# Layer 1's gathers contract over all 128 partitions, on a query block that holds rounded values in one half and the rests in the other

## The chip, the cores and the metric

The kernel runs on one core of a Trainium2 chip. A core has a matrix engine (TensorE, PE in the profile, its weight loads listed apart as PEld), a vector engine (VectorE, DVE), a scalar engine (ScalarE, ACT), GpSimd (POOL) and a queue engine for transfers (SyncE, SP). The metric is the device time of one execution in microseconds (us), the median of several runs. Lower is better.

## The reference, cut to what matters

Four layers, each `x = x + gnn(relu(layernorm(x)))`, work on x of shape 128 x 64 x 256: 128 graphs of 64 nodes with 256 features. The change touches layer 1 alone, an attention over 512 edges that are the same for all graphs:

```python
Xq = (H @ W_lin.T).reshape(bt, n, h, dh)      # 4 heads of 64
Xv = (H @ W_val.T).reshape(bt, n, h, dh)
Qs = Xq[:, src]                               # 512 edges
Kt = Xq[:, dst]
e = jnp.einsum('behd,hd->beh', jax.nn.leaky_relu(Qs + Kt, 0.2), a)
e = e + jnp.log(A0[src, dst] + EPS)[None, :, None]
attn = softmax of e over the edges that share a source node
Y = segment_sum(attn * Xv[:, dst], src)       # back to 64 nodes
return Y @ W_out.T
```

For every graph the kernel thus needs, per edge, the sum of two query rows. It gets it with a matrix multiplication by a table of zeros, ones and twos with one column per edge.

## The kernel before, in words

The 8192 tokens (128 graphs of 64 nodes) lie in 64 tiles of 128 tokens, so a tile holds two graphs: one on partitions 0 to 63, one on 64 to 127. Four tiles are a chunk, two tiles a pair `q`, eight pairs a group. Layer 1 loops over the 32 pairs in `edges(q)`. For each of the two tiles of a pair it does this:

- `gather(it)` takes the tile's query block and multiplies it with `sd_hot` [128, 512], the table of edges, which stands twice, once for each half of the partitions. For each of two halves `c` of the 256 features a PSUM pair of banks gets one bank per graph (`par`). ScalarE evicts the pair with a ReLU into `lr` (L1131).
- `project(it + 2)` makes the query block of the tile two further on: eight passes on TensorE at L1090, four into a bank `p` for 256 query features and 4 sums per head (`QS` = 260), four into a bank `pv` for the values. The products are in fp32, which TensorE does in two recorded passes each. The gather's are in fp32r, one pass, which rounds; so the query is split into a rounded piece and the rest, both fp32r, and both are gathered. ScalarE writes the rounded piece `xq[:, 0, :]` by a cast from PSUM (L1098), VectorE the rest `xq[:, 1, :]` by a subtraction (L1099). GpSimd adds the 4 columns of head sums of both pieces into `head_sums` (L1103).
- `joined` lets VectorE fold the two feature halves (`scalar_tensor_tensor`, L1137).

Between the tiles stand, in every even pair, the transposes of the next chunk's normalised rows (`turn1`, L173, two halves of four transposes with a PSUM bank each, evicted by ScalarE at L176), and at the end of a pair the score of the pair before it (L1146). After eight pairs `linear_part` (L1162) adds the part of the leaky ReLU that is linear, from `head_sums`, and the softmax of that group of pairs (`edge_softmax`) is worked off in small steps on VectorE during the next pairs, one to three steps a pair. The last eight pairs also carry the multiplication with the values (`weigh`, `put_out`).

PSUM has eight banks: two pairs for the gathers (`pair_bank`), and four single ones (`bank`). Of the four, one holds a group's scores, one the values `pv` of two tiles, and the others go to `p` and to the transposes in turn.

The order on each engine is laid out by a planner when the program is built; `late(...)` marks an instruction that keeps its place in the program's order. Buffers that matter: `xq` has 4, `lr` 6, `head_sums` 2.

A matmul on 64 partitions uses half the rows of TensorE's array, and two on opposite halves run side by side. That is the form of the gathers here: for each feature half, the two pieces one after the other accumulate in PSUM, and the two graphs run side by side.

Of the kernel before, what the change touches and what calls it, by code (L numbers as in the profile page):

```python
# [9 lines left out]
F32 = mybir.dt.float32  # L10
# [4 lines left out]
ALU = mybir.AluOpType  # L15
AX = mybir.AxisListType

P = 128
T = 64
D = 256  # L20
HEADS = 4
# [10 lines left out]
def gnn_stack_kernel(ctx: ExitStack, tc: tile.TileContext, a: dict, out: bass.AP):  # L32
    nc = tc.nc
# [10 lines left out]
    def bank():  # L44
        return psums["now"].tile([P, 512], F32, tag="bank", name="bank", bufs=psums["banks"])

    def pair_bank():
        return psums["now"].tile([P, 2, 512], F32, tag="pair", name="pair", bufs=2)
# [29 lines left out]
    def late(ins):  # L78

        tc.keep_in_program_order(ins)  # L80
# [192 lines left out]
    sd_hot = tabs.tile([P, E], F32R, tag="sd_hot", name="sd_hot")  # L273
# [205 lines left out]
    with ExitStack() as l0:  # L479
# [39 lines left out]
        with ExitStack() as conv:  # L519
# [38 lines left out]
            for h in range(2):  # L558
                r = slice(h * T, (h + 1) * T)
# [4 lines left out]
            p = bank()  # L564
# [366 lines left out]
        for slot in range(len(tasks) + 2):  # L931
# [26 lines left out]
            if new:  # L958
                next(one)
                flight.append((new, one))  # L960
                at, k = new[0], new[2]
# [38 lines left out]
    with ExitStack() as l1:  # L1000
# [4 lines left out]
        def pool(name, bufs):  # L1005
            return l1.enter_context(tc.tile_pool(name=name, bufs=bufs, reuse_waits="tile"))
# [12 lines left out]
        sgp = pool("sgp", 2)  # L1019
# [7 lines left out]
        QS = D + HEADS  # L1027
# [10 lines left out]
        hTs, queries, values, scores, waiting = {}, {}, {}, {}, []  # L1038
        sums_of, values_bank = {}, [None]
# [37 lines left out]
        def project(it):  # L1077

            n, i = it // 4, it % 4
            if i == 0:  # L1080
                kept = n >= NCH - KEPT
                values[n] = (later_pools["vk"] if kept else vp).tile([P, 4, D], F32, tag="xv", name="xv")
            p = bank()
            if not i % 2:
                values_bank[0] = bank()
            pv = values_bank[0]
            parts = ((p[:, :QS], slice(0, QS)), (pv[:, i % 2 * D : (i % 2 + 1) * D], slice(QS, QS + D)))
            for o, cols in parts:
                for k in range(2):
                    ins = nc.tensor.matmul(  # L1090
                        o, hTs[n][:, k, i * P : (i + 1) * P], wlv[:, k, cols], start=k == 0, stop=k == 1
                    )
                    if k == 0:
                        late(ins)


            xq = queries[it] = t3.tile([P, 2, QS], F32R, tag="xq", name="xq")
            nc.scalar.copy(xq[:, 0, :], p[:, :QS])  # L1098
            late(nc.vector.tensor_tensor(xq[:, 1, :], p[:, :QS], xq[:, 0, :].bitcast(F32), ALU.subtract))  # L1099
            g, at = it // 16, it % 2 * 32 + it % 16 // 2 * HEADS  # L1100
            if g not in sums_of:
                sums_of[g] = sgp.tile([P, T], F32, tag="head_sums", name="head_sums")
            nc.gpsimd.tensor_tensor(  # L1103
                sums_of[g][:, at : at + HEADS], xq[:, 0, D:].bitcast(F32), xq[:, 1, D:].bitcast(F32), ALU.add
            )
            if i % 2:
                (nc.vector.tensor_copy if i > 2 else nc.scalar.copy)(
                    values[n][:, i - 1 : i + 1, :].rearrange("p i d -> p (i d)"), pv
                )
            if i == 3 and n < NCH - KEPT:  # L1110
                nc.sync.dma_start(out=xv_mem[n], in_=values.pop(n))

        def gather(it):

            lrs = []
            for c in range(2):
                p = pair_bank()
                for piece in range(2):
                    for par in range(2):
                        r = slice(par * T, (par + 1) * T)  # L1120
                        ins = nc.tensor.matmul(  # L1121
                            p[:, par, :],
                            queries[it][r, piece, c * P : (c + 1) * P],
                            sd_hot[r, :],
                            start=piece == 0,
                            stop=piece == 1,
                        )
                        if not par and not piece:
                            late(ins)
                lr = lrp.tile([P, 2, E], F32, tag="lr", name="lr")  # L1130
                nc.scalar.activation(lr, p, AF.Relu)  # L1131
                lrs.append(lr)
            return lrs
# [23 lines left out]
        def linear_part(g):  # L1157

            s = sums_of.pop(g)
            for par in range(2):  # L1160
                r = slice(par * T, (par + 1) * T)
                ins = nc.tensor.matmul(  # L1162
                    scores[g][r, :], s[r, :], sd_hot[r, :].bitcast(F32), start=False, stop=True, skip_group_check=True
                )
                if not par:
                    late(ins)
# [266 lines left out]
        def next_score():  # L1433
            q, lrs = waiting.pop(0)
            score(q, lrs)
            if q % 8 == 7:
                linear_part(q // 8)
                behind.append(edge_softmax(q // 8))
# [7 lines left out]
        def edges(q):  # L1446

            n, odd = q // 2, q % 2
            it = 2 * q
            halves = gather(it)  # L1450
            last_out()
            if it + 2 < NT:
                project(it + 2)
# [9 lines left out]
            for _ in range(2 if odd else 1):  # L1463
                step_behind()
            halves = gather(it + 1)
            last_out()
            if it + 3 < NT:
                project(it + 3)
# [18 lines left out]
        for it in range(2):  # L1487
            project(it)
# [765 lines left out]
```

## Time and profile before

| | |
|---|---|
| median of 3 runs | 1962.27 us (1961.59 to 1963.83) |
| the profiled execution | 1963.89 us, of which the span of instructions is 1962.1 us |
| layer 1's gathers, first and last start | 1256.0 and 1518.4 us of the span |
| gather matmuls (L1121) | 512, of 64 rows and 512 columns |
| projections (L1090) | 480 recorded passes, mean 393 ns each |
| cast of the query (L1098, ScalarE) | 64, mean 381 ns |
| subtraction (L1099, VectorE) | 64, mean 420 ns |
| fold (L1137, VectorE) | 64, mean 1299 ns |
| ReLU of the gathered rows (L1131, ScalarE) | 128, mean 1022 ns |
| head sums (L1103, GpSimd) | 64, from 191 to 1173 ns |

How to read the lines: a timeline line gives the start and the length in us of a run of equal instructions, the engine, the source line, the operation, the tile it writes and those it reads, the shape, the count, and in brackets the idle time of the engine ahead of it and what ended that. Matmuls overlap, so the time that a run of them takes is the distance to the start of the next run rather than its length. A group line ends in busy time, mean length in ns, and idle time ahead of the group.

### The profile page before, as it was taken

The numbers are of one execution on the slowest core, as the hardware profiler recorded it, in microseconds if no ns is written. First come the engines' busy times: TensorE is split into PE (matmuls) and PEld (weight loads), VectorE is DVE, ScalarE is ACT, GpSimd is POOL, SyncE is SP. The second block draws the span as 40 slices with busy tenths as digits, with TensorE's granted clock in tenths as the row PEclk, the third lists the DMA queues.
The fourth block names the chain that finished last, engine by engine and source line by source line (L and its number), as shares of the span: only waits on it lengthen the run. The fifth ranks groups of instructions, "written<-read, shape, count | busy, mean of one in ns | idle before, by whom it ended". The sixth has DMA issues, their size and how long they took to land. (4 is left out here: it accounts for less than half of the span.)

```text
span 1962.1 us, 25581 instructions
## 1 busy us (share of the span) xinstructions
PE 1930.9 (98%) x9406; PEld 1388.7 (71%) x9406; DVE 1305.4 (67%) x2458; ACT 1145.3 (58%) x2153; POOL 459.6 (23%) x614
## 2 busy tenths in 40 slices
PE   9999999999999999999999999999999999999998
PEld 7777478866678874788666888766656775534787
DVE  8774675574475567765654755657766777787887
ACT  4353775564565547665654656567666556592554
POOL 3000031040030011320400200256665420000574
PEclk9999999999999999999999999999999999999999
DMA  7512000010010044000100100441333841022112
GB/s 267 178 59 97 0 22 1 1 44 0 1 43 1 1 161 140 22 1 0 44 0 1 43 1 17 165 137 68 111 134 124 318 159 57 1 65 86 44 65 87
DMA packets 63870, 135.61 MB, mean 69 GB/s; under 512 B 6656, under 2 KB 41344, under 8 KB 61440
## 3 DMA queue, kind: packets, MB, share of 16 engines
q1 hardware_dynamic: 59808, 124.33, 18.4%
q0 software_dynamic: 3328, 9.44, 1.3%
q8 instruction: 74, 1.21, 0.2%
q14 instruction: 52, 0.43, 0.1%
q10 hardware_dynamic: 608, 0.20, 0.1%
HBM read 87.55 MB, written 46.40 MB: 68 GB/s over the span
## 5 line engine op out<-in xcount | busy, mean ns | idle before, releaser
L767 ACT ACTIVATE gate<-gate,bias 128x256 f32<-128x256 f32 (+2 forms) x368 | 247.2, 678 | 176.0 <-DVE gate L783 94.1
L739 PE MATMUL pa<-xop,sih 128*128 128x256 f32 (+2 forms) x1056 | 342.4, 417 | 4.6 <-DVE gate L793 4.4
L739 PEld LDWEIGHTS pa<-xop,sih 128*128 128x128 f32 x1056 | 198.4, 190 | 75.8 <-issue 18.9
L739 PE MATMUL pc<-xop,wih 128*128 128x256 f32 (+2 forms) x736 | 251.1, 423 | 0.0
L783 DVE TENSOR_TENSOR gate<-pb,gate 128x256 f32<-128x256 f32 (+2 forms) x184 | 87.5, 475 | 224.5 <-PE pb L739 152.3
L739 PE MATMUL pa<-lstm_h,shh 128*128 128x256 f32 (+1 forms) x672 | 212.7, 398 | 0.0
L739 PEld LDWEIGHTS pc<-xop,wih 128*128 128x128 f32 x736 | 139.8, 190 | 51.2 <-issue 22.5
L800 DVE TENSOR_TENSOR gate<-pc,gate 128x256 f32<-128x256 f32 (+2 forms) x184 | 87.4, 475 | 111.9 <-PE pc L739 111.4
L1131 ACT ACTIVATE lr<-pair 128x1024 f32<-128x1024 f32 x128 | 124.1, 1022 | 63.7 <-PE pair L1121 35.1
L739 PEld LDWEIGHTS pa<-lstm_h,shh 128*128 128x128 f32 x672 | 127.7, 190 | 30.2
L739 PE MATMUL pc<-lstm_h,whh 128*128 128x256 f32 (+1 forms) x448 | 141.8, 398 | 0.0
L782 ACT COPY gate<-pa 128x256 f32<-128x256 f32 (+2 forms) x184 | 76.1, 413 | 85.6 <-PE pa L739 85.1
L1090 PE MATMUL bank<-wlv,hT 128*128 128x260 f32 x480 | 120.2, 393 | 0.0
L793 DVE TENSOR_TENSOR gate<-pa,gate 128x256 f32<-128x256 f32 (+2 forms) x184 | 87.4, 475 | 41.4 <-PE pa L739 40.7
L767 ACT ACTIVATE gate<-pa,bias 128x256 f32<-128x256 f32 (+2 forms) x184 | 93.9, 510 | 30.8 <-PE pa L739 29.0
L1090 PEld LDWEIGHTS bank<-wlv,hT 128*128 128x128 f32 x480 | 86.3, 189 | 31.4 <-issue 14.7
L787 ACT COPY gate<-pa 128x256 f32<-128x256 f32 (+2 forms) x184 | 75.3, 409 | 56.3 <-PE pa L739 55.3
L739 PE MATMUL pa<-xop,wih 128*128 128x256 f32 (+1 forms) x320 | 101.6, 399 | 1.3 <-ACT xop L718 1.2
L739 PE MATMUL pb<-xop,wih 128*128 128x256 f32 (+1 forms) x320 | 100.6, 398 | 0.0
L739 PEld LDWEIGHTS pc<-lstm_h,whh 128*128 128x128 f32 x448 | 85.1, 190 | 20.1
L506 POOL TENSOR_TENSOR shh<-whh 128x512 f32<-128x512 f32 x6 | 7.8, 1294 | 378.9 <-DMA whh<-in_WhhT 321.0
L790 ACT COPY gate<-pc 128x256 f32<-128x256 f32 (+2 forms) x136 | 57.9, 426 | 53.1 <-PE pc L739 52.4
(377 smaller groups left out, 3968.9 us busy)
## 6 DMA issues: line engine op xcount, KB each, us to landing
field<-keep SPq DMA_DIRECT2D x4, 2304.0 KB
wih<-in_WihT SPq DMA_DIRECT2D x8, 1024.0 KB
xres<-in_x SPq DMA_DIRECT2D x16, 512.0 KB
xa<-xres POOLq DMA_DIRECT2D x16, 512.0 KB, 7.9
dense<-field SPq DMA_DIRECT2D x4, 2048.0 KB
xin<-xb SPq DMA_DIRECT2D x16, 512.0 KB
h<-xb SPq DMA_DIRECT2D x16, 512.0 KB
xin<-in_x SPq DMA_DIRECT2D x15, 512.0 KB
```

Source lines behind the costliest of these rows:

```text
L506: keep(nc.gpsimd.tensor_tensor(o, x, y, op))
L739: ins = nc.tensor.matmul(p[:, : self.N], weights[kind, self.phase](k, q), x[k], start=first_ and kind == "ih", stop=kind == "hh" or not se ...
L767: nc.scalar.activation(out, in_, AF.Tanh if q == 2 else AF.Sigmoid, bias=bias[:, self.w - 1, 2 * q + j : 2 * q + j + 1],)
L782: nc.scalar.copy(blk[0, 0], pa[:, :N])
L783: nc.vector.tensor_tensor(blk[0, 0], pb[:, :N], blk[0, 0], ALU.add)
L787: nc.scalar.copy(blk[1, 0], pa[:, :N])
L790: (nc.vector.tensor_copy if not self.t and self.w > 1 else nc.scalar.copy)(blk[1, 1], pc[:, :N])
L793: nc.vector.tensor_tensor(blk[1, 1], pa[:, :N], blk[1, 1], ALU.add)
L800: nc.vector.tensor_tensor(blk[1, 0], pc[:, :N], blk[1, 0], ALU.add)
L1090: ins = nc.tensor.matmul(o, hTs[n][:, k, i * P : (i + 1) * P], wlv[:, k, cols], start=k == 0, stop=k == 1)
L1131: nc.scalar.activation(lr, p, AF.Relu)
```

## The change

A query block still has two parts, but they are now one per graph rather than one per piece. The part of the first graph (`par` 0) holds that graph's rounded values in its own half of the partitions, 0 to 63, and the rests of the same values in the other half, 64 to 127; the part of the second graph holds them the other way round. Because the table of edges stands in both halves, one matmul over all 128 partitions sums the rounded values and the rests of one graph at once, so four matmuls of 128 rows take the place of eight of 64.

To fill the block, ScalarE casts the PSUM bank into both parts (260 elements become 520), and VectorE then overwrites the foreign half of each part with the rests: two subtractions on 64 partitions each, whose result is written to the other half of the partitions than the one it was read from. The head sums are kept as they are in the two parts (GpSimd copies 2 x 4 columns in place of an addition of 4), `head_sums` is twice as wide, and the linear part contracts over 128 partitions too.

```diff
             xq = queries[it] = t3.tile([P, 2, QS], F32R, tag="xq", name="xq")
-            nc.scalar.copy(xq[:, 0, :], p[:, :QS])
-            late(nc.vector.tensor_tensor(xq[:, 1, :], p[:, :QS], xq[:, 0, :].bitcast(F32), ALU.subtract))
+            nc.scalar.copy(xq, p[:, :QS].unsqueeze(1).to_broadcast([P, 2, QS]))
+            for par in range(2):
+                own, other = (slice(h * T, (h + 1) * T) for h in (par, 1 - par))
+                late(nc.vector.tensor_tensor(
+                    xq[other, par, :], p[own, :QS], xq[own, par, :].bitcast(F32), ALU.subtract
+                ))
             g, at = it // 16, it % 2 * 32 + it % 16 // 2 * HEADS
             if g not in sums_of:
-                sums_of[g] = sgp.tile([P, T], F32, tag="head_sums", name="head_sums")
-            nc.gpsimd.tensor_tensor(
-                sums_of[g][:, at : at + HEADS], xq[:, 0, D:].bitcast(F32), xq[:, 1, D:].bitcast(F32), ALU.add
-            )
+                sums_of[g] = sgp.tile([P, 2, T], F32, tag="head_sums", name="head_sums")
+            nc.gpsimd.tensor_copy(sums_of[g][:, :, at : at + HEADS], xq[:, :, D:].bitcast(F32))
...
                 p = pair_bank()
-                for piece in range(2):
-                    for par in range(2):
-                        r = slice(par * T, (par + 1) * T)
-                        ins = nc.tensor.matmul(
-                            p[:, par, :],
-                            queries[it][r, piece, c * P : (c + 1) * P],
-                            sd_hot[r, :],
-                            start=piece == 0,
-                            stop=piece == 1,
-                        )
-                        if not par and not piece:
-                            late(ins)
+                for par in range(2):
+                    ins = nc.tensor.matmul(
+                        p[:, par, :], queries[it][:, par, c * P : (c + 1) * P], sd_hot, start=True, stop=True
+                    )
+                    if not par:
+                        late(ins)
...
                 ins = nc.tensor.matmul(
-                    scores[g][r, :], s[r, :], sd_hot[r, :].bitcast(F32), start=False, stop=True, skip_group_check=True
+                    scores[g][r, :], s[:, par, :], sd_hot.bitcast(F32), start=False, stop=True, skip_group_check=True
                 )
```

## The prediction

> **What bounds the kernel now.** I read the page first: TensorE (PE) is busy for 98% of the span at full granted clock, and nothing on the chain that ended last touches layer 1. So layer 1 counts as far as it shifts PE's row.
>
> ```profile
> PE 1930.9 (98%) x9406; PEld 1388.7 (71%) x9406; DVE 1305.4 (67%) x2458; ACT 1145.3 (58%) x2153; POOL 459.6 (23%) x614
> ```
>
> Then the timeline of PE over one pair of tiles. Its lines are merged, so I read the start of one to the start of the next.
>
> ```profile
> 1382.52 1.06 PE L1146 MATMUL bank<-lr,afield 128*32 128x512 f32 x8
> 1383.51 1.21 PE L1121 MATMUL pair<-sd_hot,xq 64*128 64x512 f32 x8
> 1384.65 2.01 PE L1090 MATMUL bank<-wlv,hT 128*128 128x260 f32 x8
> 1386.49 1.29 PE L173 MATMUL bank<-ident,h 128*128 128x128 f32 x8
> 1387.71 1.20 PE L1121 MATMUL pair<-sd_hot,xq 64*128 64x512 f32 x8
> 1388.85 2.01 PE L1090 MATMUL bank<-wlv,hT 128*128 128x260 f32 x8
> 1390.79 1.06 PE L1146 MATMUL bank<-lr,afield 128*32 128x512 f32 x8
> ```
>
> A gather G (L1121) takes 1.14 us, a score S 0.99. A projection P takes 1.84 between a gather and the transposes T, 1.94 between a gather and a score. The chain of waits prices the same 128-row passes, undisturbed, in layer 4:
>
> ```profile
> 1837.02 0.87 PE pair L1958 x8
> 1837.90 3.50 PE bank L51 x16
> ```
>
> That is 0.218 us a pass and 0.109 a transpose. P's eight passes are 1.74, so P pays 0.10 on entry from the gather's 64-row shape, and 0.10 more when it leaves for another shape. By the same count a gather is 0.10 + four row-tiled pairs + 0.10, a pair 0.234.
>
> Next the timelines of ScalarE, VectorE, the weight loads and (last line, a later pair) PE:
>
> ```profile
> 1384.34 1.94 ACT L1131 ACTIVATE lr<-pair 128x1024 f32<-128x1024 f32 x2 [1.14 <-PE pair L1121]
> 1386.17 0.38 ACT L1098 CAST xq<-bank 128x260 fp32r<-128x260 f32 x1
> 1386.58 0.43 DVE L1099 TENSOR_TENSOR xq<-bank,xq 128x260 fp32r<-128x260 f32 x1 [1.42 <-ACT xq L1098]
> 1387.13 0.42 PEld L173 LDWEIGHTS bank<-ident,h 128*128 128x128 f32 x4 [0.27 <-issue]
> 1469.85 0.63 PE L173 MATMUL bank<-ident,h 128*128 128x128 f32 x4 [0.55 <-DVE xq L1099]
> ```
>
> The second half of T (call it T2) starts 0.11 us after the subtraction ends, and the last line names that subtraction: T2 needs the PSUM bank that the query leaves. So in a pair with transposes (every even one) a chain over ScalarE and VectorE holds PE already.
>
> Last the busy time by stage, for three pairs in which a softmax is worked off, and one without (columns: length, then PE, weight loads, DVE, ACT, POOL):
>
> ```profile
> 1336.87:1345.14 8.27, 8.21 (x52) 5.31 (x48) 7.10 (x15) 6.66 (x9) 4.20 (x6) 1.00 0.19 63
> 1345.14:1352.28 7.14, 7.14 (x45) 4.38 (x42) 7.11 (x10) 5.84 (x9) 5.42 (x6) 1.00 0.18 73
> 1352.28:1360.55 8.27, 8.21 (x53) 5.31 (x49) 7.48 (x17) 5.65 (x8) 4.49 (x8) 1.00 0.20 66
> 1376.37:1383.51 7.14, 7.14 (x44) 4.39 (x41) 3.84 (x5) 5.00 (x7) 6.69 (x10) 1.00 0.30 91
> ```
>
> VectorE is full (7.11 of 7.14) in the second of them.
>
> **The change, part by part.** *Gathers.* Eight 64-row matmuls become four of 128 rows, of P's own shape. No row shows a 128-row fp32r pass of 512 columns. Lower bound 0.216 (P's slot, an equal stream), upper 0.234 (the pair, which already streams 128 partitions of fp32r at once); I take 0.225. The shape changes G to P, P to G and T to G vanish; S to G and P to S stay. A pair without T goes from 7.14 to 1.00 + 1.74 + 0.90 + 1.84 + 1.00 = 6.48 (-0.66); one with T (0.87) would go from 8.27 to 7.35 (-0.92). Fifteen of each, 0.66 for pair 30 and 0.3 for the last, which only gathers: -24.7 us.
>
> The Trainium skill ("TensorE: Matmul & The Clock Gate", Part 3, The mechanism) speaks against this: weight loads overlap running matmuls only where the row groups differ, as they do between the present half tiles. By that rule each 128-row pass would pay its 0.19 us load as well, four a gather, some 48 us over 63 gathers, an estimate. But P's slot of 0.218 leaves no room for a load of 0.19 in front of each pass, so I let loads hide.
>
> *Subtraction.* One 128-partition instruction (0.43, the next starting 0.345 behind it) becomes two on 64 partitions across halves. These rows, by shape, say that half the partitions save nothing, and what halves of other quadrants do:
>
> ```profile
> L2079 DVE COPY field<-bank 64x256 f32<-64x256 f32 x1 | 0.4, 417 | 1.1 <-PE bank L2073 1.1
> L790 DVE COPY gate<-pc 128x256 f32<-128x256 f32 x36 | 14.9, 414 | 2.1 <-PE pc L739 1.8
> 147.63 0.45 DVE L253 TENSOR_TENSOR bdH<-bank,anT 64x64 f32<-64x64 f32 x2
> ```
>
> The two halves at L253 take 0.206 and 0.228 and together 0.45, so they do not overlap, and 0.013 lies between. Bounds for the next full instruction: 0.085 before the second half's end (as now), or 0.013 behind it; I take the latter, by the rows of halves. VectorE gains 2 x 0.443 - 0.345 = 0.54 us a tile (lower bound 0.345). The skill ("VectorE: DVE Perf Modes", Two Vector instructions with no wait between them) holds any instruction whose start quadrant differs from the last one's, so that fold too; no row here shows a full instruction behind a shifted half.
>
> *Cast.* 260 to 520 elements: 0.38 to 0.60, by the 128x512 copy from PSUM at L1107 (0.588). ScalarE has room (5.00 + 0.43 of 6.48).
>
> *T2.* First fold-relu starts 0.83 behind the gather (stays: the second pass now begins 0.325 in, before 0.34), cast 1.83 later, then 0.60 + 0.03 + 0.87 + 0.11: T2 at 4.27 instead of 1387.13 - 1383.51 = 3.62. The pair then ends after 0.44 + 0.90 + 1.84 + 1.00 = 8.45: +0.18 instead of -0.92. So 1.10 is lost in each of 15 pairs: +16.5. Should T2 be given the bank that T's first half leaves, it waits for that copy (till about 4.1) and 2.5 us of this come back.
>
> *VectorE in the softmax pairs.* From the subtraction at 1332.80 to that at 1355.37 it idles only 1.03 (1343.22 to 1344.25, for a projection). Its 21.5 of work gain 6 x 0.54: 24.8, begun 3.28 into the stretch, which makes T2 of the fourth pair 3.28 + 24.8 + 0.98 = 29.0 instead of 26.15. After it 0.48 is saved. The four pairs grow by 2.4 where the sums above give -1.0: 3.4 lost, in two groups of eight pairs; in the third the values' matmuls lengthen PE's row (the pair from 1474.5 takes 11.9) and I take 1.5. +8.3, and 0.3 in the second pair, where the layer-0 outputs load VectorE.
>
> *Small ones.* The first gather waits for both halves where half of it ran ahead: 0.5. The linear part stays two column halves side by side (1.01 now): 0, bounds 0.1 either way, three in the loop. POOL's sum becomes a copy of 8 elements, 0.2 to 1.16 us like now; POOL's fullest pair has 6.69 of 7.14, its neighbour 6.19 of 8.26, and its normalised rows are wanted half a chunk later; if that cover went, T's first half would be late. DMAs and SP's queue are untouched.
>
> Sum: -24.7 + 16.5 + 8.3 + 0.3 + 0.5 = +0.9. The profiled execution took 1963.9 (span 1962.1), which would be 1964.8; it stood 1.6 over the median of 1962.27, so I say 1963.2. A measurement of this kernel tells about 0.2%, 3.9 us, from no change.
>
> **The rivals.** *Faster:* VectorE isn't the bound. For: its order may be laid out anew, with scans in gaps; against: the 7.11 of 7.14. Without the 8.3, with a 0.216 pass (63 x 0.036 = 2.3) and the cheaper bank (2.5): 1950; with the 8.3 alone gone 1955. If T2 didn't wait either, 1938.
>
> *Slower:* VectorE binds wider. One mechanism, decided from about 0.4 us more lost per pair in 12 softmax pairs than I count: the exponential (ScalarE, L1181) sits ahead of a cast and waits for VectorE, so the delays add. The idle 1.03 stays in three groups (3), the third group costs as much as the others (1.9), the pass is 0.234 (2.3): 1970 to 1972.
>
> *The pass isn't single.* A 128-row fp32r pass that costs what fp32 passes of 512 columns cost (57.8 us for 128 at L51, 0.45): 63 x 0.9 = 57 more, 2018. Against: the pairs stream the same bytes in 0.234.
>
> **How the numbers follow.** No measurable change 0.35; faster 0.28 (0.02 of it 1938); VectorE wider 0.33; double pass 0.04. The range leaves out the double pass, the 1938 and the tails: 1949 to 1976.
>
> **What would show it.** Right: gathers at 0.9 to 1.0 us, P at 1.74 before a gather, T2 starting near 4.3 behind its gather on "DVE xq", pairs without T near 6.5, VectorE without idle in the softmax pairs. Wrong: a T2 that doesn't wait, or pairs without T above 7.

## The result and the profile after

The changed kernel takes 1966.1 us (median of 22 runs, 1963.5 to 1972.5) against 1961.8 us (22 runs, 1961.0 to 1964.9) before: a ratio of 1.0022, 95% interval 1.0016 to 1.0028, or 3.1 to 5.5 us slower. The prediction was 1963.2, in a range of 1949 to 1976. The profiled execution took 1968.6 us with a span of 1966.8.

The page's row of busy times:

```profile
PE 1914.2 (97%) x9150; PEld 1393.2 (71%) x9150; DVE 1344.5 (68%) x2522; ACT 1156.8 (59%) x2153; POOL 457.2 (23%) x614
```

TensorE has 16.7 us less work than before (1930.9), VectorE 39.1 us more. TensorE's work fell and the span didn't: what was saved is idle time now. The timeline of one even pair of tiles shows where (start, length, engine, line, operation; in brackets the idle time ahead and what ended it), first PE, then ScalarE, then VectorE:

```profile
1388.88 1.06 PE L1142 MATMUL bank<-lr,afield 128*32 128x512 f32 x8
1389.88 1.20 PE L1121 MATMUL pair<-sd_hot,xq 128*128 128x512 f32 x4
1390.91 1.90 PE L1090 MATMUL bank<-wlv,hT 128*128 128x260 f32 x8
1392.65 0.60 PE L173 MATMUL bank<-ident,h 128*128 128x128 f32 x4
1394.03 0.63 PE L173 MATMUL bank<-ident,h 128*128 128x128 f32 x4 [0.78 <-ACT hT L176]
1394.41 1.17 PE L1121 MATMUL pair<-sd_hot,xq 128*128 128x512 f32 x4
1395.42 1.91 PE L1090 MATMUL bank<-wlv,hT 128*128 128x260 f32 x8
1397.26 1.07 PE L1142 MATMUL bank<-lr,afield 128*32 128x512 f32 x8
...
1392.52 0.60 ACT L1098 CAST xq<-bank 128x520 fp32r<-128x520 f32 x1
1393.29 0.60 ACT L176 ACTIVATE hT<-bank 128x512 f32<-128x512 f32 x1 [0.17 <-PE bank L173]
...
1393.15 0.86 DVE L1101 TENSOR_TENSOR xq<-bank,xq 64x260 fp32r<-64x260 f32 x2 [0.65 <-ACT xq L1098]
1394.05 1.29 DVE L1133 SCALAR_TENSOR_TENSOR lr<-lr,fold 128x1024 f32<-128x1024 f32 x1
```

A gather now takes 1.03 us (1389.88 to 1390.91) where it took 1.14. The second half of the transposes T (T2) starts 4.15 us behind its gather where it started 3.65 behind, after 0.78 us of waiting. It waits for ScalarE's copy of T's first half (L176), which ends at 1393.89, and not for the subtractions, which end at 1394.01, only 0.02 ahead of it: its weight load starts 0.11 us behind the copy's end, as before the change it started 0.11 behind the subtraction's. So the planner has given T2 the bank that T's first half leaves.

The timeline of the softmax pairs 12 and 13 (PE):

```profile
1357.20 1.90 PE L1090 MATMUL bank<-wlv,hT 128*128 128x260 f32 x8
1360.08 0.63 PE L173 MATMUL bank<-ident,h 128*128 128x128 f32 x4 [0.98 <-DVE xq L1101]
1361.48 0.63 PE L173 MATMUL bank<-ident,h 128*128 128x128 f32 x4 [0.78 <-ACT hT L176]
...
1370.74 0.52 PE L1195 MATMUL bank<-ident,e 128*128 128x128 f32 x3 [2.06 <-DVE e L1189]
```

and the busy time by stage, one line per pair 10 to 13 (length, then PE, weight loads, DVE, ACT, POOL):

```profile
1340.26:1349.64 9.38, 7.86 (x45) 5.35 (x41) 9.11 (x17) 7.13 (x9) 3.02 (x4) 1.00 0.19 57
1349.64:1356.16 6.52, 6.52 (x36) 4.61 (x32) 6.28 (x9) 6.15 (x9) 5.62 (x7) 1.00 0.20 80
1356.16:1365.74 9.58, 7.82 (x45) 5.27 (x41) 9.36 (x15) 5.94 (x8) 4.77 (x5) 1.00 0.19 57
1365.74:1374.96 9.22, 7.16 (x41) 4.92 (x37) 8.37 (x15) 5.34 (x7) 6.29 (x11) 1.00 0.14 58
```

VectorE fills the even ones (9.11 of 9.38, 9.36 of 9.58). It now holds PE at three places: T (0.98), the projection ahead of the score (0.74 in pair 10), and the transposes of the softmax itself (L1195), which stand still for 2.06 us until VectorE has multiplied `e` with the reciprocals (L1189). From the first gather to pair 30's, PE stands still for 20.8 us in waits of over 0.15 us where it stood still for 2.6: 11.8 of them end with ScalarE's copy (L176), 3.7 with a subtraction and 4.3 with `e`.

Taking the starts of the gathers from the trace, pair by pair, before and after differ so (us; "undisturbed" means without a stretch of reduced clock, which comes below):

| part | predicted | measured |
|---|---|---|
| first gather with pairs 0 and 1 | +0.3 | +0.1 |
| 7 odd pairs without softmax work | -4.6 | -4.2 |
| 7 even pairs without softmax work | +1.3 | +0.9 |
| softmax pairs 10 to 13 | +2.4 | +3.5 |
| softmax pairs 18 to 21 | +2.4 | +3.5 |
| pairs 24 to 29 (values) | +0.1 | -1.1 |
| pair 30, last gather and end of layer 1, undisturbed | -1.0 | -0.5 |
| sum (of the unrounded rows) | +0.9 | +2.0 |

The row of pair 30 is taken against the second profile of before, below; in the first one a ReLU (L1131) holds a gather of pair 30 for 0.72 us, and from pair 30 to the end of layer 1 it takes 2.3 us more. The second profile of the same kernel, below, gives the same numbers to 0.05 in the first four rows and in that of the pairs 24 to 29, and +3.7 for the second softmax group. The rest of the 4.3 us isn't in any row. Two things bear on it. First, the profiles shift against each other ahead of layer 1, where no instruction differs: by 5.2 us in the first profile after (one VectorE instruction of layer 0, L852 at 1097.41, took 4.82 us there instead of 1.33), by 0.2 the other way in its repetition, by up to 1.8 between two profiles of before. Second, the granted clock: over 22 executions after, its mean is 0.9981, over the 27 executions of before that ran beside the later experiments 0.9996. After's times go with it: 1964.7 (median of 5) at 0.999, 1966.0 (13) at 0.998, 1969.2 (2) at 0.997, 1972.5 at 0.996; one run at 1.000 took 1966.2. A mean lower by 0.0015 is at most some 3 us of TensorE's time at full speed, worked out as 0.0015 x 1965. It doesn't say where in the kernel the clock was low: in the first profile after, the two stretches at half clock lie in layer 0, behind the long L852 (from 1104.2 us), and at the very end of the span (from 1964.3), none in layer 1.

### The profile page after: what moved, and what is told of

Same layout as the page of the kernel before. It is cut to its first block, busy times and chain, and to the rows that moved or that the text cites. A ratio compares the mean times of both kernels' runs of the same rounds, so it can differ in the third digit from the quotient of the medians.

```text
span 1966.8 us, 25221 instructions
## 1 busy us (share of the span) xinstructions
PE 1914.2 (97%) x9150; PEld 1393.2 (71%) x9150; DVE 1344.5 (68%) x2522; ACT 1156.8 (59%) x2153; POOL 457.2 (23%) x614
## 3 DMA queue, kind: packets, MB, share of 16 engines
q8 instruction: 72, 1.18, 0.3%
## 5 line engine op out<-in xcount | busy, mean ns | idle before, releaser
L1090 PE MATMUL bank<-wlv,hT 128*128 128x260 f32 x480 | 114.8, 382 | 1.8 <-DVE xq L1101 1.8
```

The costliest lines, as they stand in the source:

```text
L1090: ins = nc.tensor.matmul(o, hTs[n][:, k, i * P : (i + 1) * P], wlv[:, k, cols], start=k == 0, stop=k == 1)
```

## The experiments

**The changed kernel and the kernel before once more.** Nothing is edited; these say how far two profiles of the same kernel differ.

> The changed kernel once more, unaltered. Theory (the sum of the prediction): inside layer 1's loop, from the first gather to the last, it takes 0 to 2 us more than before, whatever the run. Of the 4.7 us of span that the first profile shows, 5.2 had gathered before the first projection of layer 1, 4.2 of it at one VectorE instruction of layer 0 (L852, 4.82 us instead of 1.33). If that was chance, this profile has L852 near 1.3 us there and a median 1962 to 1964; rival: the changed kernel brings it on in every run, L852 is long again, and the median is 1965 to 1967.

> The kernel before once more, unaltered: 1962 to 1963, a ratio of 1.000, and a second trace of it. Question to it: does the load of the values that holds PE for 1.2 to 2.5 us near the end of layer 1 in the changed kernel's traces (at 1566 to 1570) also hold it here in some runs, and does the clock fall to half inside layer 1? Theory: neither (both come from the changed order).

Measured: 1966.4 after, 1.0018 [1.0009, 1.0027]; 1962.1 before, 0.9999 [0.9990, 1.0008]. The loop comes out as expected, and L852 is short again (1.27 us), so its 4.8 us were chance; but the median is the rival's and not the 1962 to 1964 that was to go with a short L852. From the first gather to pair 30's, the two profiles after take 252.1 and 252.3 us, the two of before 250.9 and 250.9. In the repetition after, the clock falls inside layer 1. Busy time by stage around pair 20 of that profile (the column behind the five engines is the granted clock):

```profile
1418.00:1420.00 2.00, 1.18 (x6) 0.70 (x4) 1.97 (x4) 2.00 (x3) 0.60 (x2) 1.00 0.37 35
1420.00:1422.00 2.00, 1.05 (x9) 0.87 (x9) 1.93 (x5) 0.60 (x2) 1.23 (x1) 1.00 0.58 227
1422.00:1424.00 2.00, 2.00 (x8) 1.60 (x7) 1.90 (x5) 1.76 (x3) 0.00 (x0) 0.61 0.00 0
1424.00:1426.00 2.00, 2.00 (x7) 1.59 (x6) 1.93 (x5) 1.30 (x2) 1.24 (x1) 0.53 0.00 0
```

and its timeline of PE there:

```profile
1420.17 0.63 PE L173 MATMUL bank<-ident,h 128*128 128x128 f32 x4 [0.98 <-DVE xq L1101]
1421.57 0.63 PE L173 MATMUL bank<-ident,h 128*128 128x128 f32 x4 [0.78 <-ACT hT L176]
1421.96 1.64 PE L1121 MATMUL pair<-sd_hot,xq 128*128 128x512 f32 x4
1423.39 3.13 PE L1090 MATMUL bank<-wlv,hT 128*128 128x260 f32 x8
1426.45 1.06 PE L1142 MATMUL bank<-lr,afield 128*32 128x512 f32 x8
```

PE is idle for 1.8 of four microseconds, then runs at about half clock: the projection at 1423.39 takes 3.06 us to the next start where it takes 1.84 elsewhere. The clock's record shows half speed for 3.4 us. Pair 20 grows by 1.6 to 11.2 us, but pair 21 gives 1.4 of it back, because VectorE has caught up by then (its wait at L1195 falls from 2.2 to 0.8): among VectorE's waits the fall is nearly free. A second fall, from 1565.8 us, follows a wait for the load of the values:

```profile
1565.99 1.99 PE L1312 MATMUL pair<-att,xv_in 64*64 64x64 f32 x64 [2.45 <-DMA xv_in<-xv]
```

From pair 30 on the repetition takes 2.7 us more to the end of layer 1 than the first profile, 1.3 of it in this longer wait (2.45 for 1.18), which leaves 1.4 for the fall. The same two waits at pair 20 stand in the first profile after without a fall, so a wait of that size allows it and doesn't force it (the last section says what goes with a fall). Neither profile of before has such a stretch in layer 1; but the load of the values holds PE for 1.39 us (at 1564.74) in the second of them too, so that wait, against what was expected, isn't of the changed order.

**One half of the change alone.** `gather_only` has the new gathers and linear part on the block that the old preparation leaves, so a matmul sums other pieces than it should:

```diff
-            nc.scalar.copy(xq, p[:, :QS].unsqueeze(1).to_broadcast([P, 2, QS]))
-            for par in range(2):
...
+            nc.scalar.copy(xq[:, 0, :], p[:, :QS])
+            late(nc.vector.tensor_tensor(xq[:, 1, :], p[:, :QS], xq[:, 0, :].bitcast(F32), ALU.subtract))
```

> The 128-row gathers with the old preparation of the query (one cast of 260, one subtraction on 128 partitions): the part that saves, alone. Its gathers add up the wrong values; nothing else is changed. Theory: the transposes' second half starts near 3.6 us behind its gather as before, pairs with transposes take 7.8 instead of 8.27, pairs without 6.5 instead of 7.14, so 15 x 0.47 + 15 x 0.66 + 1 = 18 us less than before: 1944 (1940 to 1949). Rival, the saving isn't in the shape of the matmuls or is lost elsewhere than in the preparation: 1958 to 1966.

`prep_only` keeps the old gathers and head sums and prepares the block as the change does, with the wide cast and two subtractions, but each writes its own half, so the values are those of before:

```diff
+            nc.scalar.copy(xq, p[:, :QS].unsqueeze(1).to_broadcast([P, 2, QS]))
+            for par in range(2):
+                own = slice(par * T, (par + 1) * T)
+                late(nc.vector.tensor_tensor(
+                    xq[own, 1, :], p[own, :QS], xq[own, 0, :].bitcast(F32), ALU.subtract
+                ))
```

> The old 64-row gathers behind a preparation of the new cost: the cast writes both parts (520 elements), and the subtraction is two instructions on 64 partitions each (written to the half they are read from, since the old gathers need the rests there). The part that costs, alone. Theory: the second half of the transposes starts 0.65 later in 15 pairs (10 us), VectorE holds the softmax pairs of three groups for 4 more, the first gather for 0.5: 1976 (1971 to 1981). Rival, the preparation is hidden: 1961 to 1966.

Measured: `gather_only` 1951.7, 0.9939 [0.9925, 0.9953]; `prep_only` 1982.9, 1.0105 [1.0090, 1.0120]. From first gather to pair 30's they differ from before by -13.2 and +19.8. Both times lie above their ranges: each half of the change moves the time the way that was said of it, but the gathers alone bring less than expected and the preparation alone costs more, and together the two come to +1.2 where their sum is +6.6. The even pair of `gather_only` says why, in the timeline of PE:

```profile
1287.93 1.20 PE L1117 MATMUL pair<-sd_hot,xq 128*128 128x512 f32 x4
1288.97 1.90 PE L1090 MATMUL bank<-wlv,hT 128*128 128x260 f32 x8
1290.71 0.60 PE L173 MATMUL bank<-ident,h 128*128 128x128 f32 x4
1291.57 0.63 PE L173 MATMUL bank<-ident,h 128*128 128x128 f32 x4 [0.26 <-DVE xq L1099]
```

T2 starts 3.64 behind its gather, as before the change, since the chain to the old subtraction has its old length; only the parts behind T2 get shorter. In the softmax pairs `gather_only` wins 0.9 us in four pairs where the gathers by themselves are worth 3.2, because VectorE was already full there. So about half of what the gathers are worth by themselves was not to be had at all, whatever the preparation cost. In `prep_only` the same chain holds PE the other way:

```profile
1295.37 0.63 PE L173 MATMUL bank<-ident,h 128*128 128x128 f32 x4 [0.74 <-ACT hT L176]
```

Its first softmax group takes 7.9 us more than before, with waits of 2.3 and 2.7 us for the subtraction.

**One of the two subtractions left out.** The part of the second graph keeps rounded values in both halves, so its rests are missing:

```diff
-            for par in range(2):
+            for par in range(1):
```

> The changed kernel with one of the two subtractions left out (the block of the second graph holds its rounded values twice): 0.45 us of VectorE less a tile, 29 us in all, and the bank is free that much earlier. Theory (VectorE holds the softmax pairs): the pairs with a softmax lose the idle time of PE that waits for DVE xq and DVE e, 4 to 6 us, the others change little since their wait is on ScalarE: 1961 (1958 to 1964). Rival, VectorE isn't what holds PE: within 2 us of the changed kernel's 1966.

Measured: 1953.3, 0.9959 [0.9945, 0.9972]; 12.8 us under the changed kernel, where 1958 to 1964 was expected. Timeline of PE and VectorE in an even pair:

```profile
1289.00 1.20 PE L1121 MATMUL pair<-sd_hot,xq 128*128 128x512 f32 x4
...
1292.84 0.63 PE L173 MATMUL bank<-ident,h 128*128 128x128 f32 x4 [0.47 <-DVE xq L1101]
...
1292.27 0.42 DVE L1101 TENSOR_TENSOR xq<-bank,xq 64x260 fp32r<-64x260 f32 x1 [1.07 <-ACT xq L1098]
1292.73 1.30 DVE L1133 SCALAR_TENSOR_TENSOR lr<-lr,fold 128x1024 f32<-128x1024 f32 x1
```

Half of the partitions cost VectorE as much as all of them: 0.42 us, and the fold starts 0.46 behind the subtraction's start. Here T2 does wait for the subtraction, 0.15 behind its end. In the even pairs T2 wins 0.31. The larger part is the softmax pairs: pairs 10 to 13 take 0.1 us more than before, where they took 3.5 more, and the transposes of the softmax no longer wait. The second subtraction is thus the larger part of what the preparation costs: the loop takes 237.7 us in `gather_only`, 240.8 here and 252.1 in the changed kernel, so 11.3 of 14.4 us come with it. Whether they come from VectorE's load or from the query's bank, which is free earlier here, this run alone doesn't tell.

**The transposes moved.** `turn_moved` puts them behind the pair's second gather, `turn_first` ahead of the first (except in pair 0):

```diff
@@ turn_moved
             if not odd:
-                turn1(n + 1)
                 sums1(n + 2, (2, 3))
...
             halves = gather(it + 1)
+            if not odd:
+                turn1(n + 1)
             last_out()
             if it + 3 < NT:
@@ turn_first
             it = 2 * q
+            if not odd and q:
+                turn1(n + 1)
             halves = gather(it)
+            if not q:
+                turn1(n + 1)
...
             if not odd:
-                turn1(n + 1)
                 sums1(n + 2, (2, 3))
```

> The changed kernel with the transposes of an even pair put behind the pair's second gather instead of ahead of it, so that the query's bank has been free for about a microsecond when their second half wants it. Theory: the wait of 1.1 us in 15 pairs goes, less what VectorE's load in the softmax pairs takes back (3): 1953 (1948 to 1957). Rival, the wait only moves to the next instruction that wants a bank (the projection behind the transposes): 1962 to 1967.

> The changed kernel with the transposes of an even pair put ahead of the pair's first gather (in the first pair behind it). There two banks are long free and ScalarE waits for the gather anyway. In the changed kernel's traces their second half idles PE for 0.78 us in every even pair until ScalarE has copied the first half out of its bank. Theory: this idle time goes in the pairs without a softmax (even pairs 7.4 to 7.6 instead of 8.38 us); in the softmax pairs VectorE holds PE and part comes back: 12 us less than the changed kernel, 1954 (1950 to 1959). Rival, the wait finds another place as it did with the transposes behind the second gather: 1963 to 1968.

Measured: `turn_moved` 1969.5, 1.0032 [1.0020, 1.0045]; `turn_first` 1966.4, 1.0022 [1.0013, 1.0031]. In both the rival held, in `turn_moved` with more than its price. There the wait goes to the projection that follows the transposes, and is longer:

```profile
1293.10 1.27 PE L1121 MATMUL pair<-sd_hot,xq 128*128 128x512 f32 x4
1294.21 1.22 PE L173 MATMUL bank<-ident,h 128*128 128x128 f32 x8
1296.43 2.01 PE L1090 MATMUL bank<-wlv,hT 128*128 128x260 f32 x8 [1.01 <-ACT hT L176]
```

In `turn_first` the waits are gone where no softmax runs: an even and an odd pair together take 13.9 us where they took 14.9. But the transposes now want their rows, which GpSimd normalises, a projection and a gather earlier, and in the loaded pairs they aren't there yet (the second line), beside other waits:

```profile
1349.36 0.73 PE L1121 MATMUL pair<-sd_hot,xq 128*128 128x512 f32 x2 [0.94 <-ACT lr L1127]
...
1354.44 0.98 PE L173 MATMUL bank<-ident,h 128*128 128x128 f32 x4 [1.02 <-POOL h L130]
...
1367.19 1.09 PE L1195 MATMUL bank<-ident,e 128*128 128x128 f32 x4 [2.59 <-DVE e L1189]
```

The clock falls to half in four places of layer 1 of this profile, and its mean over 12 executions is 0.9969, the lowest of all kernels here. Moving the transposes in all pairs gains nothing on balance.

**The same move in the kernel before.** The edit is `turn_first`'s.

> The kernel before with the transposes put ahead of the pair's first gather. The second half's short wait for the subtraction (0.25 us in 15 pairs) goes, a change of the array's shape stays: 4 us less, 1958 (1955 to 1960). If the new place is bad in itself (the normalised rows late, a bank wait in the projection) it is slower than 1962, and the run of the changed kernel with it has to be read against that.

Measured: 1961.7, 0.9999 [0.9990, 1.0008]: no difference where 1958 was expected, and its loop is 0.4 us shorter. Before the change PE stood still for only 0.06 us ahead of T2 in the plain pairs, so there was little to win: a plain even and odd pair take 15.3 us together where they took 15.4. And the new place has waits of its own, of 0.3 to 0.6 us for GpSimd's rows in pairs 3, 15 and 23.

**The copy of the values on ScalarE alone.** A chunk has two copies of values from PSUM, one for two tiles each. Before and after, VectorE does the second of them; here ScalarE does both:

```diff
-                (nc.vector.tensor_copy if i > 2 else nc.scalar.copy)(
+                nc.scalar.copy(
```

> The changed kernel with all copies of the values out of PSUM on ScalarE (before, the second of each chunk is VectorE's, 16 x 0.68 us). Theory (VectorE's load decides): leaving out a subtraction (28 us of VectorE) gave 13 us, so 10.9 us give about 5: 1961 (1958 to 1964). Rival, what counted in that run was the earlier release of the query's bank, not VectorE's load: 1965 to 1968, since ScalarE is longer before the transposes' copies.

Measured: 1961.5, 0.9995 [0.9986, 1.0004], as expected: 5 us under the changed kernel and equal to before. Busy time by stage for pairs 11 to 13:

```profile
1346.72:1353.64 6.92, 6.81 (x37) 4.53 (x33) 6.71 (x9) 6.75 (x9) 6.53 (x9) 1.00 0.20 78
1353.64:1362.05 8.41, 7.63 (x45) 5.35 (x41) 8.15 (x16) 6.42 (x9) 3.52 (x4) 1.00 0.22 63
1362.05:1370.65 8.60, 7.20 (x40) 4.92 (x36) 7.63 (x14) 5.34 (x7) 7.40 (x11) 1.00 0.15 61
```

Pair 12 takes 8.41 instead of 9.58 with VectorE 1.2 us less busy, pair 13 8.60 instead of 9.22; pair 11 gives 0.4 back. Over the loop that is 4.4 us. T2's wait of 0.78 is unchanged in the even pairs, so the two costs are separate, and the rival, that only an earlier free bank had counted in `one_rest`, is out: VectorE's load costs time by itself. The mean clock over 11 executions is 0.9995.

**More taken off VectorE.** On top of that, the last product of the softmax goes to ScalarE in four pieces in all groups, and the transposes of the softmax come two steps later; once with the change, once without:

```diff
             late(nc.vector.tensor_tensor(e, e, run, ALU.mult))
             yield
             if g < NGR - 1:
+                yield
+                yield
                 yield
...
-            if g == NGR - 1:
+            if True:
                 for ec in range(NE):
                     late(nc.scalar.activation(
```

> The same, and for the softmax: its last product (0.7 us a group) on ScalarE in four pieces as the last group has it, and its transposes two steps later, so that PE does not stand ahead of VectorE's reciprocals (idle for 2.1 us in two groups in the changed kernel, DVE e). Theory: the idle time that ends with DVE e goes (4 us) and the rest of the softmax pairs' falls: 1957 (1953 to 1961). Rival: the softmax's work only runs later into pairs that then wait: 1961 to 1966.

> The kernel before with the same two alterations, as a measure for the run above: before, VectorE was no bound (PE idles under 2 us inside the loop), so within 2 us of 1962. If it gains as much as the changed kernel does, the gathers' change has no part in it.

Measured: 1964.5, 1.0013 [1.0005, 1.0022], and 1968.8, 1.0042 [1.0030, 1.0055]. `lighter` falls to its rival, and `before_lighter` misses its expectation by 5 us. Pair 13 of `lighter` takes 6.98 us, so the wait at the softmax's transposes is gone, but these now hold a bank on into a pair that has T as well, and T waits there:

```profile
1373.81 0.63 PE L173 MATMUL bank<-ident,h 128*128 128x128 f32 x4 [1.34 <-DVE xq L1101]
1375.21 0.63 PE L173 MATMUL bank<-ident,h 128*128 128x128 f32 x4 [0.78 <-ACT hT L176]
```

In the kernel before, the same place waits too, 0.50 and then 0.78. So the later transposes cost in both kernels. How much of the loss is theirs isn't shown: the two alterations weren't run apart, T2 waits another 1.36 us for a subtraction in pair 12 of `before_lighter`, and in both the last linear part waits for GpSimd's head sums (2.50 us in `lighter`, 1.27 in `before_lighter`), as in no other profile.

**The transposes ahead only where no softmax runs.** This joins what worked: `xv_scalar`, and in pairs 4, 6 and 8 the transposes ahead of the first gather.

```diff
             it = 2 * q
+            first = q in (4, 6, 8)
+            if first:
+                turn1(n + 1)
             halves = gather(it)
...
             if not odd:
-                turn1(n + 1)
+                if not first:
+                    turn1(n + 1)
```

> The changed kernel with the values copied on ScalarE alone, and with the transposes ahead of the pair's first gather in three pairs without a softmax (4, 6 and 8). With the values on ScalarE alone these pairs took 8.38, 8.38 and 9.39 us of their own, 0.78 of it a wait at the second half of the transposes, and the pairs behind them 6.54, 6.54 and 6.52: 45.7 us for the six. With the transposes ahead in all pairs the same six took 6.52, 7.37, 6.52, 7.39, 7.53 and 7.38, 42.7. If the wait is gone there and nothing takes its place, as in those pairs, 3 us are saved: 1958.5 (1957 to 1960). If VectorE's softmax pairs behind them take the gain back, or GpSimd's normalised rows are late ahead of the transposes, 1961.5 or more.

Measured: 1957.2 us (12 runs), 0.9975 [0.9966, 0.9984]: 4.3 us below before and 8.9 below the changed kernel. Timeline of PE in pair 5 (from the gather at 1296.80) up to the transposes of pair 6:

```profile
1296.80 1.21 PE L1121 MATMUL pair<-sd_hot,xq 128*128 128x512 f32 x4
1297.84 1.90 PE L1090 MATMUL bank<-wlv,hT 128*128 128x260 f32 x8
1299.39 1.28 PE L1121 MATMUL pair<-sd_hot,xq 128*128 128x512 f32 x4
1300.51 1.90 PE L1090 MATMUL bank<-wlv,hT 128*128 128x260 f32 x8
1302.34 1.07 PE L1142 MATMUL bank<-lr,afield 128*32 128x512 f32 x8
1303.34 1.09 PE L173 MATMUL bank<-ident,h 128*128 128x128 f32 x8
1304.18 1.19 PE L1121 MATMUL pair<-sd_hot,xq 128*128 128x512 f32 x4
```

The eight transposes run in one piece, 0.84 us from start to start, with no wait anywhere. The transposes of pair 4 now fall into pair 3. Pairs 3 to 9 take 49.3 us where `xv_scalar`'s took 52.3, the 3 us expected. The mean clock is 0.9997.

## Why the prediction was right, point by point

The sum said +0.9 us and the range 1949 to 1976; 1966.1 lies 2.9 over the forecast. The range is 27 us wide and holds a gain, no change and a loss, so that it was met says little by itself. The likeliest case by the prediction's own bound of 0.2% was "no measurable change", and the interval of 0.16% to 0.28% straddles that bound, with its middle just past it. The mechanism was right in most of its places; sizes were off, and what ends T2's wait and one wait in the softmax pairs were wrong.

- *The pass is single, and loads hide.* Right. A 128-row pass takes 0.233 us from start to start (a gather's passes after the first start at 1383.681, 1383.914 and 1384.147, the projection behind them at 1384.378). I had taken 0.225 between 0.216 and 0.234, so the upper end was true: +2.0 us over 63 gathers of four. This ends the rival of the double pass, and the rule of the Trainium skill that was weighed ("TensorE: Matmul & The Clock Gate", Part 3, The mechanism): weight loads of 0.188 us, 128 rows behind 128 rows, hide behind the running matmul here, and the 48 us that the rule would have made are not there.
- *Shape changes at 0.10 us.* Right in the sum: a projection between two gathers takes 1.55 us and the gather behind it 1.12, 2.67 together against 2.64 predicted, though each alone is off by 0.2 (1.74 and 0.90 were predicted), and a pair without transposes 6.54 against 6.48.
- *T2 is late.* Right in place and size: its first weight load, from which the sum counted, starts 4.12 us behind the gather instead of 4.27, a pair with transposes 8.38 instead of 8.45. The step that was wrong is what ends the wait. The bank came from T's first half, the case that the prediction named with "till about 4.1" and left out of its sum; "on DVE xq", which it named as a sign of being right, is not what the trace shows in the plain pairs. I had put 2.5 us on that case; it brought 0.07 a pair in 7 plain pairs, 0.4 us, since the wait behind a 0.60 copy is nearly as long as the one behind the subtractions.
- *The subtraction's price on VectorE.* Right: two halves start 0.436 us apart and the fold 0.463 behind the second, 0.90 a tile, against 0.345 before; +0.55 for +0.54. The fold starts 0.03 us behind the end of the second half, where before it started 0.08 ahead of the subtraction's end. The Trainium skill ("VectorE: DVE Perf Modes", Two Vector instructions with no wait between them) states that an instruction whose start quadrant differs from the last one's is held until that has ended, and the runs agree: it shows in `prep_only`, whose halves don't cross over, and in `one_rest`, with one half, so it comes from starting at another partition, not from crossing.
- *Softmax pairs.* Right in kind, too small: +3.5 a group for +2.4. Two errors stand against each other in it. VectorE's chain up to the fourth pair (pair 12) was too dear: pairs 10 to 12 grow by 1.8 us where the sum has 3.1. The step that failed is what comes behind, "after it 0.48 is saved": the delay doesn't end with T2 of the fourth pair; it goes on to the softmax's transposes in pair 13, which wait 2.06 us for VectorE's last product, so that pair 13 grows by 1.65 where the sum has -0.66. That wait isn't in my chain, which followed only `xq`.
- *Third group and values.* I put 1.5 of loss on it; it shows 0.3 (-1.1 measured, where the plain sums give -1.4).
- *First gather.* The gather waits 1.24 us where the second half of it waited 0.57, and starts 1.27 to 1.31 later behind the last work of layer 0, in all eight profiles here that have the new gather and the new block. With the saving in pairs 0 and 1 that comes to +0.1, near enough to the +0.3 of the sum.
- *Edits at nothing.* GpSimd's copies of head sums take 1.23 us where the additions took 1.16, and no wait of PE names them in the profile after; the linear part takes 1.01 us as before (1528.26 to 1529.27).
- *What wasn't in the sum.* The granted clock. I read 1.00 in before's rows and took it for given, but with idle stretches of 1 to 2.5 us in PE's row one of the two profiles of the changed kernel runs part of layer 1 at half speed. The mean clock of 0.9981 against 0.9996 goes with up to 3 us, and the measured 4.3 lies 2.3 over the +2.0 of the undisturbed rows. Whether that rest is clock isn't shown: the shifts ahead of layer 1 are of the same size, the first profile after has no fall in layer 1, and the fall in pair 20 of the repetition was nearly free.
- *The rivals.* "VectorE binds wider" had the right cause: taking VectorE's copies away brings 5 us, one subtraction 13. Its own mechanism doesn't show: in pair 11 the exponential (L1177, 1349.84 to 1350.47) ends as the ReLU is due, and the cast comes 2.65 us behind the gather, as in a plain pair. Its price was too high at +8, mostly because the third group didn't come. The faster rival needed VectorE to have room, and `gather_only` shows that even the old subtraction left too little.

That the sum came so near is in part luck; it was nearer than its two large terms were. I booked -24.7 for the gathers and +24.8 for T2 and VectorE; the loops of the runs of the halves alone say -13.2 and +19.8, with 5.4 of overlap. Both chains existed before the change, so part of the -24.7 was never on offer, and the same part was booked again as a cost.

## What to carry to other kernels

When a change takes work off a full engine and puts some on another, follow the second engine's chain through every wait that stands on it, up to the last consumer and not only to the tile that was changed: here the softmax's own transposes stood behind the subtractions. Before counting a saving, ask in which pairs the saved engine was already close to waiting; in those it is worth nothing, and the waits that open there can also cost clock. A wait that an order creates is worth moving only where the operands of the moved step are ready: moving it in three idle pairs brought 3 us, moving it everywhere brought none.

## What was not expected of the hardware

- The clock falls to half for stretches of 3.4 us (once 6.8) inside a busy loop: in layer 1 at 1422 and 1566 us in the repetition after, at four places in `turn_first`, at two each in `prep_only` and `turn_moved`, at one each in `gather_only` and `lighter`; none in layer 1 of the first profile after, of those of before, `before_turn_first`, `before_lighter`, `one_rest`, `xv_scalar` or `free_first`. The same waits don't always bring it. The traces show what goes with it: in every profile with several such stretches, their starts lie a whole number of 3.413 us apart. With each profile cut into windows of that length on the grid of these starts, PE was idle for 1.76 to 2.55 us in the window ahead of each of these 12 falls (and of the one at 1104 us). In all other windows of the 14 profiles from 20 to 1940 us it was idle for 1.97 at most, and in only two of them for more than 1.76. So a fall goes with a window that is idle for about half of its length, and a wait that two windows share brings none: 2.84 us in `prep_only`, up to 1436.5, lie with 1.50 and 1.34 us in two of them. The Trainium skill ("TensorE: Matmul & The Clock Gate", Part 1, What's actually happening) names an idle window of some 3.4 us as what leads to the slow state; here, ahead of the fall at 1422 us, PE was idle for 1.76 of the 3.41, in two pieces of 0.98 and 0.78.
- A 128-row pass of 512 columns in fp32r takes 0.233 us, two row-tiled 64-row passes side by side 0.234: the change of form saves nothing per byte streamed, only the changes of shape around it (0.10 us each).
- VectorE's subtraction on 64 partitions takes as long as on 128 (0.42 us), and starting at another partition costs about 0.12 us more in front of the next instruction.
